# Moving the second weights' extremes from the front into the row loop, and quantizing in half pieces

## The chip, the cores and the metric

The kernel runs on one core of a Trainium2 chip. The metric is the device time of one execution in microseconds. Three runs of the kernel before took 2254.0, 2258.8 and 2258.85 us; the median is 2258.8 us. One further execution was profiled; it took 2269.5 us.

## The reference

The input is eight images of 256 channels and 56 x 56 points. Layer 0 normalizes `x` in groups of eight channels, computes from it a 7 x 7 kernel for every point and each of 16 groups (an involution), applies it and adds the result to `x`. Layer 1 normalizes again, and applies two 3 x 3 convolutions with batch norm and residuals. Both convolutions have ternary weights, and these are what the change is about:

```python
def ternary_quantize(x):
    mx, mn = (jnp.max(x), jnp.min(x))
    lo = mn + (mx - mn) / 3
    hi = mx - (mx - mn) / 3
    return jnp.where(x < lo, -1.0, jnp.where(x > hi, 1.0, 0.0)).astype(x.dtype)

def noised_tri_conv(x, w):
    tw = w - jnp.mean(w)
    tq = ternary_quantize(tw)
    out = lax.conv_general_dilated(x, tq, ...)
    center = tq[:, :, 1, 1]
    extra = lax.stop_gradient(jnp.einsum("bchw,oc->bohw", x, center))
    return out + extra
```

Each weight tensor (256 x 256 x 3 x 3, 2.36 MB) needs its mean, its maximum and its minimum before any of its values can be quantized. The quantized weights are first used by the convolutions, after layer 0 is complete.

## The kernel before, in words

The kernel has three stages: layer 0 (`ph1`), the two convolutions (`ph2`, one after the other) and a final pass over all images (`ph4`). The change touches only `ph1`.

**The row loop.** Layer 0 works through 32 quarters: eight images `b` of four quarters `c` of 64 channels. A quarter has ten rows `ty` of tiles, so the loop has 320 rows. For a row, TensorE multiplies the tiles `q` of the input with the kernels `a` of this quarter (`apply_row`, L815, PSUM tile `pa`), ScalarE and VectorE bring the result out (L827 and L828, tile `inv`), and GpSimd adds it to `x` in place (L831). In the same row, `generate` makes one or two of the fourteen units of the next quarter's `a`: TensorE matmuls into `pg` (L782), ScalarE (L786) and VectorE (L791) add the bias `bt` and write `a`. `pg` has two PSUM homes. Tiles `q` come half from a DMA (L742, four homes, fetched four rows ahead, each waiting for the row whose home it takes) and half from a transpose in TensorE (L749). Further steps are spread over the rows: the statistics of the next image (`gn1_stats`) and of this one (`gn2_stats`), both L150; loads of the next image (L545); stores of the finished one (L843); the shifted copies of the next image (`prep`, with stores at L708); and `params`, which computes the normalization of the next image from row 20 of its predecessor on, one step at each of two places in a row, with the bias matmul `br` (L576) and the addition `brn` (L579) as its last two steps.

**The order.** `pin` fixes the order of every engine's instructions to that of the text. DMAs on SyncE (SP) are in the order of the text too: one that waits holds up those behind it. Some DMAs are put into the list `tasks` and issued by `transfer(2)` at the start of the next row.

**Extremes.** Before the loop, in the front, both weights are loaded into one large tile `wf` (L631), which later is a home of `a`. `extremes` takes each weight tensor in six pieces of 768 columns: VectorE reduces to maximum (L208) and minimum (L209), ScalarE to the sum (L210). Then come small reductions, two matmuls and a transpose that bring the values of the 128 partitions together (L213 to L230), and the thresholds (L232 to L245). Behind the loads of `wf`, SP writes zeros from the tile `xn` to the borders of the scratch tensors `xtd` (L637); GpSimd writes the first shifted copy of image 0 into the same `xn` (L674), so it waits for these.

**Quantization.** From row 8 of the loop on, `quantize` takes one step in every row. Each weight tensor is taken in sixteen pieces of 3 x 96 columns. A piece has one home in SBUF and takes seven rows: fetch (L257), the two comparisons (L261, L262) two rows later, the subtraction and first combination (L264 to L277) in the next, then five more combinations of 96 columns in two rows (L279 to L284), and a store of six planes through `tasks` (L287). Both tensors take 224 rows.

Of the kernel before, what the change touches and what calls it, by code (L numbers as in the profile page):

```python
# [80 lines left out]

QN, QJ = 96, 3 * C // 96
QS = WT
SLOT = (0, 2, 3, 4, 5, 1)
QM = 6


@with_exitstack
def involution_tri_block_kernel(
# [102 lines left out]
    def piece_of(pool, name):  # L192
        return pool.tile([P, (4 + QS) * QN], F32, tag="piece", name=f"piece_{name}")

    def extremes(w, cols, pool, transposer, psum_tile, name):

# [6 lines left out]

        s, mx, mn = col(QM), col(QM), col(QM)
        f = nf // QM
        for j in range(QM):
            v = w[:, j * f:(j + 1) * f]
            nc.vector.tensor_reduce(mx[:, j:j + 1], v, AX.X, ALU.max)  # L208
            nc.vector.tensor_reduce(mn[:, j:j + 1], v, AX.X, ALU.min)  # L209
            nc.scalar.activation(v, v, AF.Identity, accum_out=s[:, j:j + 1])  # L210
            yield
        sums, ends = col(), col(2)
# [5 lines left out]
        nc.vector.memset(v[:, :P], 1.0)  # L218
        yield

        ps = psum_tile(f"ends_{name}")
        nc.tensor.matmul(ps[:, P:P + 1], v[:, :P], sums, start=True, stop=True)
        nc.tensor.transpose(ps[:2, :P], ends, transposer)
        mean, top = cols[:, 0:1], col()
        nc.vector.tensor_scalar(mean, ps[:, P:P + 1], 1.0 / (P * nf), None, ALU.mult)
        nc.vector.tensor_reduce(top[:2], ps[:2, :P], AX.X, ALU.max)
        nc.vector.tensor_copy(v[:2, P:2 * P], top[:2].to_broadcast([2, P]))
        yield
        ps = psum_tile(f"all_{name}")
        nc.tensor.transpose(ps[:, :2], v[:2, P:2 * P], transposer[:2, :2])  # L230
        ex = col(2)
        nc.vector.tensor_copy(ex, ps[:, :2])  # L232
# [4 lines left out]

        d, q0, r, th = (col() for _ in range(4))
        nc.vector.tensor_tensor(d, amx, amn, ALU.subtract)
# [7 lines left out]

    def quantize(dst, w_dram, cols, pool, tasks, name):


        mean, lo, hi = (cols[:, k:k + 1] for k in range(3))
        for t in range(CT):
            for j in range(QJ):
                v = piece_of(pool, name)
                w, u = v[:, :3 * QN], v[:, 3 * QN:]
                o = (t * QJ + j) * 3 * QN
                nc.sync.dma_start(w, w_dram[:, o:o + 3 * QN])  # L257
                yield
                yield
                g = u[:, :3 * QN]  # L260
                nc.vector.tensor_scalar(g, w, mean, hi, ALU.subtract, ALU.is_gt)  # L261
                nc.vector.tensor_scalar(w, w, mean, lo, ALU.subtract, ALU.is_lt)  # L262
                yield
                nc.vector.tensor_tensor(g, g, w, ALU.subtract)  # L264

                def part(x, k):
                    return x[:, k * QN:(k + 1) * QN]


                c0, c1 = max(C, j * QN) - j * QN, min(2 * C, (j + 1) * QN) - j * QN  # L270
                if c0 < c1:
                    g1 = part(u, 0)[:, c0:c1]
                    nc.vector.tensor_scalar(g1, g1, 2.0, None, ALU.mult)

                e, f = part(w, 0), part(w, 1)
                g1, g0, g2 = (part(u, k) for k in range(3))
                nc.vector.tensor_tensor(e, g0, g2, ALU.add)  # L277
                yield
                nc.vector.scalar_tensor_tensor(f, g2, 4.0, g0, ALU.mult, ALU.add)  # L279
                nc.vector.tensor_tensor(part(u, 3), e, g1, ALU.add)  # L280
                nc.vector.tensor_tensor(part(u, 4), e, g1, ALU.subtract)
                yield
                nc.vector.scalar_tensor_tensor(part(u, 5), g1, 2.0, f, ALU.mult, ALU.add)
                nc.vector.scalar_tensor_tensor(part(u, 6), g1, -2.0, f, ALU.mult, ALU.add)  # L284

                def store(u=u[:, QN:], o=t * 3 * C + j * QN):
                    nc.sync.dma_start(  # L287
                        bass.AP(dst[:].tensor, dst[:].offset + o,
                                [[QS * CT * 3 * C, P], [CT * 3 * C, QS], [1, QN]]), u)

                tasks.append(store)
                yield
                yield

# [223 lines left out]
    with ExitStack() as ph1:  # L518
# [38 lines left out]
        def params(b):  # L557


            dst = small.tile([P, NCQ, 2], F32, tag="gn1", name=f"gn1_{b}")  # L560
            yield from group_norm_params(mvs.pop(b), dst, ps_one, f"a{b}")
            for c in range(NCQ):
                nc.vector.tensor_scalar(
                    wrn[:, c, :].rearrange("p (i r) -> p i r", i=2),
                    wr[:, c, :].unsqueeze(1).to_broadcast([P, 2, CR]),
                    dst[:, c, 0:1], None, ALU.mult)

            edge = small.tile([P, 2, NCQ], F32, tag="gn1e", name=f"gn1e_{b}")
            for j in range(2):
                nc.vector.tensor_scalar(edge[:, j], dst[:, :, 1], side_sb[:, j:j + 1], None, ALU.mult)  # L570
            prm[b], prm_edge[b] = dst, edge
            yield
            ps = ps_one(f"br_{b}")
            for c in range(NCQ):
                for i in range(2):
                    nc.tensor.matmul(ps[i * CR:(i + 1) * CR, :1], wr[:CH, c, :], dst[:CH, c, 1:2],  # L576
                                     start=(c == 0), stop=(c == NCQ - 1))
            yield
            nc.vector.tensor_tensor(brn, br, ps[:, :1], ALU.add)  # L579
# [43 lines left out]
        for v in xe:  # L623
            nc.gpsimd.memset(v, 0.0)

        nf = CT * 9 * C
        wf = apool1.tile([P, A_COLS], F32, tag="a1", name="wf")
        for i, v in enumerate((w1, w2)):
            for j in range(2):
                o = j * nf // 2  # L630
                nc.sync.dma_start(wf[:, i * nf + o:i * nf + o + nf // 2], v[:, o:o + nf // 2])  # L631
        zero = xn.rearrange("p k r x -> p (k r x)")

        for d in (d for ds in xt_d for d in ds):
            for r0, n in ((0, PAD), (PAD + HH, HQ - PAD - HH)):
                e = n * QX * RP // P
                nc.sync.dma_start(  # L637
                    bass.AP(d[:].tensor, d[:].offset + r0 * QX * RP, [[e, P], [1, e]]), zero[:, :e])

        def reduce(b, py):  # L640
# [251 lines left out]
        for _ in params(0):  # L892
            pass
        strips, around = prep(0), surround(0, 0)
        a_next = matrices(0)
        thresholds = [pieces.tile([P, 32], F32, tag=f"cols{i}", name=f"cols{i}") for i in range(2)]
        ext = [extremes(wf[:, i * nf:(i + 1) * nf], thresholds[i], pieces, ident_sb, ps_one, f"w{i}")
               for i in range(2)]

        found = chain(*(islice(v, QM) for v in ext), *ext)  # L900

        for py in range(PY):
            next(strips)
            transfer(len(tasks))
            reduce(0, py)
            for _ in range(3):
                next(found)
# [25 lines left out]
        for k in rows[:QLEAD]:  # L933
            transpose_q(*k)
        pin()
        norm = iter(())
        quant = chain(*(quantize(wq_d[i], v, thresholds[i], pieces, tasks, f"w{i + 1}")
                        for i, v in enumerate((w1, w2))))
        last = None
# [197 lines left out]
```

## Time and profile before

| what | us |
|---|---|
| median of three runs | 2258.8 |
| the profiled execution | 2269.5 |
| its span, first to last instruction | 2267.7 |
| first full row of `apply_row` matmuls starts | 80.67 |
| the first convolution's matmuls start | 1155.95 |
| PE, DVE, ACT, POOL busy | 1866.4, 1706.7, 1268.3, 584.5 |
| mean granted TensorE clock | 0.924 |

The span is what the profile shows of the profiled execution; all times of single instructions count from its start. A share of busy time is a mean over stages with different limits. Where an engine is idle, the profile names the event that ended its wait. A granted clock of 0.5 means that TensorE ran at half speed. GB/s and the DMA share are means over the stretch asked for.

### The profile page before, as it was taken

The page shows a single profiled execution, that of the slowest core. Times are in us where ns is not written, and L with a number is a line of the kernel's source. Part 1 is how long each engine was busy: PE and PEld are TensorE (multiplying, and loading weights), DVE is VectorE, ACT ScalarE, POOL GpSimd, SP SyncE. Part 2 cuts the span into 40 slices and gives each one's busy share as a digit, 9 for nine tenths or more (in the row PEclk, how much of TensorE's full clock was granted, in tenths as well). Part 3 has the DMA queues.
Part 4 walks back from the last instruction along what each step waited for, and adds up shares of the span by engine and source line. Part 5 has one row for each costly group of instructions (what it writes and reads, how often), then busy time and mean ns, then how long its engine had stood idle before and what let it go on. Part 6 is the DMA issues. An engine that isn't in the chain of part 4 may idle for free.

```text
span 2267.7 us, 72706 instructions
## 1 busy us (share of the span) xinstructions
PE 1866.4 (82%) x31088; PEld 1716.6 (76%) x31088; DVE 1706.7 (75%) x2906; ACT 1268.3 (56%) x2461; POOL 584.5 (26%) x1320
## 2 busy tenths in 40 slices
PE   4889899898998989999879999999799999970000
PEld 3778777777877877778779999999799999970000
DVE  6676857667585775655689999998999999975444
ACT  3555455455554645556446766665576666673434
POOL 2545546364563645546400000000000000000000
PEclk9899999999999999999989999999899999995555
DMA  6556646566474754645453333334333333369999
GB/s 211 154 157 181 199 131 206 147 192 189 131 221 120 225 164 138 197 119 160 138 206 116 129 134 140 119 116 161 133 138 117 116 116 116 116 255 401 410 430 403
DMA packets 156447, 411.24 MB, mean 181 GB/s; under 512 B 51550, under 2 KB 62172, under 8 KB 148444
## 3 DMA queue, kind: packets, MB, share of 16 engines
q1 hardware_dynamic: 150528, 376.56, 49.9%
q10 hardware_dynamic: 5596, 30.03, 3.2%
q8 instruction: 245, 4.01, 0.8%
q14 instruction: 78, 0.64, 0.1%
HBM read 264.05 MB, written 142.48 MB: 179 GB/s over the span
## 4 chain that ended last, share of the span: by engine, by line
PE 38%; DMA 7%; DVE 3%; ACT 1%; issue 1%; ACTq 0%; SPq 0%; POOL 0%; DVEq 0%
PE c L464 37%; DMA y1f<-y1d 3%; DMA x1f<-x1d 2%; DMA out_y<-x1f 1%; DVE x1f L1064 1%; DMA y2f<-y2d 1%; ACT dummy L416 1%; DVE y1f L1062 0%; ACT y1f L1061 0%; ACT y1f L1063 0%; PE pa L815 0%; PE ptq L749 0%; DVE q L346 0%; DVE r L366 0%; DVE u L373 0%
## 5 line engine op out<-in xcount | busy, mean ns | idle before, releaser
L464 PE MATMUL c<-pl,wq 128*128 128x392 f32 x4608 | 857.1, 348 | 20.2 <-ACT pl L351 20.2
L464 PEld LDWEIGHTS c<-pl,wq 128*128 128x128 f32 x4608 | 855.1, 189 | 22.0 <-ACT pl L351 20.7
L791 DVE TENSOR_TENSOR a<-pg,bt 126x756 f32<-126x756 f32 (+3 forms) x640 | 393.2, 656 | 192.7 <-ACT a L786 147.3
L782 PE MATMUL pg<-kr,wl 64*126 64x140 f32 (+1 forms) x6144 | 459.4, 294 | 14.3 <-DVE a L791 7.1
L782 PEld LDWEIGHTS pg<-kr,wl 64*126 64x126 f32 x6144 | 396.8, 196 | 66.4 <-issue 41.5
L815 PE MATMUL pa<-a,q 126*32 126x48 f32 x17920 | 273.2, 208 | 62.3 <-issue 38.5
L815 PEld LDWEIGHTS pa<-a,q 126*32 126x32 f32 x17920 | 223.1, 111 | 115.8 <-issue 53.4
L786 ACT ACTIVATE a<-pg,bt 126x126 f32<-126x126 f32 x768 | 243.3, 475 | 102.6 <-PE pg L782 102.4
L831 POOL TENSOR_TENSOR x<-x,inv 128x168 f32<-128x168 f32 x320 | 166.4, 520 | 438.5 <-DVE inv L828 375.5
L828 DVE SCALAR_TENSOR_TENSOR inv<-pa,half_sb,inv 128x168 f32<-128x168 f32 x320 | 117.1, 366 | 171.0 <-ACT inv L827 144.8
L351 ACT CAST pl<-r 128x812 fp32r<-128x812 f32 x192 | 162.5, 868 | 145.2 <-DVE r L346 126.9
L752 ACT COPY q<-ptq 126x384 f32<-126x384 f32 x320 | 138.2, 481 | 162.7 <-issue 96.2
L331 POOL MEMSET xp<- 128x116 f32 x32 | 6.3, 195 | 829.4 <-DVE a L346 829.4
L416 ACT ACTIVATE dummy<-y,nc 128x1568 f32<-128x1568 f32 (+2 forms) x144 | 210.1, 1459 | 5.3 <-DVE y L484 3.5
L674 POOL TENSOR_SCALAR xn<-x,gn 128x224 f32<-128x224 f32 (+2 forms) x384 | 179.1, 486 | 130.0 <-PE pt L717 70.8
L352 DVE TENSOR_TENSOR pl<-r,pl 128x812 fp32r<-128x812 f32 x192 | 187.2, 1002 | 28.2 <-ACT pl L351 27.0
L674 POOL TENSOR_SCALAR xe<-x,gn 128x168 f32<-128x168 f32 (+2 forms) x384 | 161.2, 439 | 0.0
L720 ACT COPY stg<-pt 98x512 f32<-98x512 f32 x128 | 74.9, 585 | 137.0 <-issue 88.5
L749 PE MATMUL ptq<-ident_sb,xe 128*126 128x128 f32 x960 | 144.2, 285 | 4.6 <-DVE var_a L170 2.6
L150 DVE BATCH_NORM_STATS2 st<-x 128x6 f32<-128x392 f32 x256 | 138.3, 557 | 11.8 <-DMA x<-in_x 10.2
L827 ACT ACTIVATE inv<-pa,half_sb 128x168 f32<-128x168 f32 x320 | 128.2, 401 | 26.8 <-PE pa L815 25.7
L1011 ACT ACTIVATE xp<-raw,gn 128x392 f32<-128x392 f32 (+1 forms) x124 | 82.6, 721 | 62.9 <-DVE a L346 58.9
(144 smaller groups left out, 1846.2 us busy)
## 6 DMA issues: line engine op xcount, KB each, us to landing
q<-xtd SPq DMA_DIRECT2D x320, 252.0 KB
raw<-x1d SPq DMA_DIRECT2D x32, 812.0 KB
raw<-y1d SPq DMA_DIRECT2D x32, 812.0 KB
x<-in_x SPq DMA_DIRECT2D x64, 392.0 KB
xtd<-stg SPq DMA_DIRECT2D x128, 196.0 KB
x1d<-x SPq DMA_DIRECT2D x64, 392.0 KB
y1d<-y SPq DMA_DIRECT2D x30, 784.0 KB
y2d<-y SPq DMA_DIRECT2D x30, 784.0 KB
```

What stands on the lines that cost most here:

```text
L150: nc.vector.bn_stats(st[:, j, :], xt[:, j * NC:(j + 1) * NC])
L351: nc.scalar.copy(hi, r)
L352: nc.vector.tensor_tensor(lo, r, hi.bitcast(F32), ALU.subtract)
L416: nc.scalar.activation(dst, v, f, bias=shift[:, to:to + 1], accum_out=stats[:, to, j, n:n + 1])
L464: nc.tensor.matmul(ps[:, to, :NM], wq[k][:, t, dx, to * P:(to + 1) * P], part[:, t, :, dx:dx + W], start=(c == 0), stop=(c == last))
L674: nc.gpsimd.tensor_scalar(dst[:, i - d - k0:f - d - k0, :, x0:x0 + n], v[:, i:f, :, j0:j0 + n], scale, bias, ALU.mult, ALU.add)
L749: nc.tensor.transpose(pt[:NQ, k * P:(k + 1) * P], xe[c % 2][:, k, PY * ty:PY * ty + QY].rearrange("p r x -> p (r x)"), ident_sb)
L782: nc.tensor.matmul(dst, wl[rows, c, gp, o:o + NQ], kr[py][rows, px, :], start=True, stop=True)
L786: nc.scalar.activation(whole[:, g0 + i, p0 + j], ps[:NQ, i, j * nt:(j + 1) * nt], AF.Identity, bias=bt[:, c, g0 + i, p0 + j:p0 + j + 1])
L791: nc.vector.tensor_tensor(dst[:, g0:g0 + 2, p0:p0 + nv].rearrange("q g p t -> q g t p"), ps[:NQ, :, t0 * nv:t1 * nv].rearrange("q i (t p) ...
L815: nc.tensor.matmul(ps[o:o + 32, k * 2 * n:(k + 1) * 2 * n], q[:NQ, k, o:o + 32], av[:, t + k, g * 2 * n:(g + 1) * 2 * n], start=True, stop ...
L831: nc.gpsimd.tensor_tensor(xv, xv, iv.rearrange("p t (y x) -> p y t x", x=PX), ALU.add)
```

## The change

It has three parts.

1. The second weights leave the front. Only the first tensor is loaded into `wf`, and its load stands behind the zero writes in SP's order. Its six pieces go two to each of the three steps `py` in front of the first `generate`, its small steps between the first units. The second tensor's extremes stand in the loop between the quantization of the first and of the second: twelve pieces of 384 columns are fetched into the piece homes, and VectorE makes all three reductions, maximum and minimum in one row and the sum in the next. ScalarE has no part in it. Two pieces take five rows, the whole 36 steps.
2. Pieces of the quantization have 48 columns for 96, and there are two homes for one. The work of a half piece is in two rows for four: the comparisons, the subtraction and the first combination in one, the five others in the next. Two half pieces take seven rows, three rows apart, so one tensor takes 115 steps. The store is issued by SP in its place in the row and no longer through `tasks`, three rows after the last of its work on VectorE. One row after it comes the fetch into the same home.
3. `params` has one more empty step ahead of the bias matmul `br`; this and `brn` come half a row later in the text.

```diff
-QN, QJ = 96, 3 * C // 96
+QN, QJ = 48, 3 * C // 48
-QM = 6
+QM, QM2 = 6, 12
     def piece_of(pool, name):
-        return pool.tile([P, (4 + QS) * QN], F32, tag="piece", name=f"piece_{name}")
+        return pool.tile([P, (4 + QS) * QN], F32, tag="piece", bufs=2, name=f"piece_{name}")
+    def paced(events):
+        for r in range(max(events) + 1):
+            for f in events.get(r, ()):
+                f()
+            yield
...
+        def fetch(j):
+            held[j] = piece_of(pool, name)[:, :f]
+            nc.sync.dma_start(held[j], w_dram[:, j * f:(j + 1) * f])
+        def seek(j):
+            v = w[:, j * f:(j + 1) * f] if w is not None else held[j]
             nc.vector.tensor_reduce(mx[:, j:j + 1], v, AX.X, ALU.max)
             nc.vector.tensor_reduce(mn[:, j:j + 1], v, AX.X, ALU.min)
-            nc.scalar.activation(v, v, AF.Identity, accum_out=s[:, j:j + 1])
-            yield
+            if w is not None:
+                nc.scalar.activation(v, v, AF.Identity, accum_out=s[:, j:j + 1])
+        def add(j):
+            nc.vector.tensor_reduce(s[:, j:j + 1], held.pop(j), AX.X, ALU.add)
+        events = {}
+        for j in range(n):
+            if w is not None:
+                events[j] = [lambda j=j: seek(j)]
+            else:
+                r = 5 * (j // 2) + j % 2 * 2
+                events.setdefault(r, []).append(lambda j=j: fetch(j))
+                events.setdefault(r + 2, []).append(lambda j=j: seek(j))
+                events.setdefault(r + 3, []).append(lambda j=j: add(j))
+        yield from paced(events)
...
+        events = {}
+        for k in range(CT * QJ):
+            r = 7 * (k // 2) + k % 2 * 3
+            for n, f in ((0, fetch), (2, ternary), (3, planes_of), (6, store)):
+                events.setdefault(r + n, []).append(lambda f=f, k=k: f(k))
+        yield from paced(events)
...
             prm[b], prm_edge[b] = dst, edge
             yield
+            yield
             ps = ps_one(f"br_{b}")
...
-        nf = CT * 9 * C
-        wf = apool1.tile([P, A_COLS], F32, tag="a1", name="wf")
-        for i, v in enumerate((w1, w2)):
-            for j in range(2):
-                o = j * nf // 2
-                nc.sync.dma_start(wf[:, i * nf + o:i * nf + o + nf // 2], v[:, o:o + nf // 2])
         zero = xn.rearrange("p k r x -> p (k r x)")
         for d in (d for ds in xt_d for d in ds):
...
+        nf = CT * 9 * C
+        wf = apool1.tile([P, A_COLS], F32, tag="a1", name="wf")
+        for j in range(2):
+            o = j * nf // 2
+            nc.sync.dma_start(wf[:, o:o + nf // 2], w1[:, o:o + nf // 2])
...
-        found = chain(*(islice(v, QM) for v in ext), *ext)
+        found = ext[0]
         for py in range(PY):
             next(strips)
             transfer(len(tasks))
             reduce(0, py)
-            for _ in range(3):
+            for _ in range(2):
                 next(found)
...
-        quant = chain(*(quantize(wq_d[i], v, thresholds[i], pieces, tasks, f"w{i + 1}")
-                        for i, v in enumerate((w1, w2))))
+        made = [quantize(wq_d[i], v, thresholds[i], pieces, f"w{i + 1}")
+                for i, v in enumerate((w1, w2))]
+        quant = chain(made[0], ext[1], made[1])
```

In the new `quantize`, `ternary` holds the lines L261 to L277 of before, `planes_of` L279 to L284 and `store` L287, each over half as many columns.

## The prediction

> **What bounds the kernel now.** I read the page first, then the timeline of the front (0 to 90 us), then stretches of the loop, then the groups by shape and the waits. On the page:
>
> ```profile
> PE 1866.4 (82%) x31088; PEld 1716.6 (76%) x31088; DVE 1706.7 (75%) x2906; ACT 1268.3 (56%) x2461; POOL 584.5 (26%) x1320
> ```
>
> PE is the fullest engine, but the share hides three stages: a front until the first row's matmuls (80.67 us), the row loop (to 1147 us), and the two convolutions with the final pass, which the change doesn't touch. In the front PE waits for others. The timeline from 0 to 45 us (start, length, engine, line, work, idle time ahead and its releaser):
>
> ```profile
> 12.02 5.13 SPq L631 DMA_DIRECT2D wf<-in_w  x4
> ...
> 17.27 16.56 SPq L637 DMA_DIRECT2D xtd<-xn  x16
> ...
> 35.59 1.34 POOL L674 TENSOR_SCALAR xn<-x,gn 128x224 f32<-128x224 f32 x3 [31.85 <-DMA xtd<-xn]
> ...
> 36.98 1.09 PE L717 MATMUL pt<-ident_sb,xn 128*98 128x128 f32 x4 [5.59 <-POOL xn L674]
> ```
>
> Both weights (4.7 MB) go out ahead of the sixteen zero writes that read `xn`; POOL can't overwrite `xn` before these land, and PE idles 5.59 us. From 45 to 90 us:
>
> ```profile
> 56.38 0.84 ACT L210 ACTIVATE wf<-wf 128x768 f32<-128x768 f32 x1 [1.02 <-DVE cols L209]
> ...
> 59.83 0.56 PE L222 MATMUL ends_w<-cols,piece_w 128*128 128x1 f32 x2 [3.28 <-DVE piece_w L218]
> ...
> 80.67 0.80 PE L815 MATMUL pa<-a,q 126*32 126x48 f32 x54 [1.03 <-DVE a L791]
> ```
>
> The extremes of the second weights stand in the middle of this, and PE waits behind them. In the loop, two stretches of 40 rows (one image), the first with quantization, the second without (us, then PE, PEld, DVE, ACT, POOL busy, clock, DMA share, GB/s):
>
> ```profile
> 353.10:491.00 137.90, 122.93 (x3312) 104.72 (x3310) 96.67 (x237) 73.64 (x201) 72.62 (x160) 0.99 0.58 169
> ...
> 904.90:1040.10 135.20, 124.35 (x3312) 106.57 (x3310) 81.95 (x179) 72.97 (x201) 69.95 (x160) 0.96 0.55 157
> ```
>
> PE is at 90%. Quantization adds 14.7 us to DVE and 2.7 us to the image: most of it hides behind PE, not all.
>
> **What the Trainium skill says.** Its page "TensorE: Matmul & The Clock Gate", part 1, says that an idle window of about 3.4 us halves the PE clock. The trace agrees: after the 5.59 us gap the record has 0.5 from 33.8 to 40.6 us, and again from 57.7 to 64.5 us around the 3.28 us gap. "VectorE: DVE Perf Modes", on the TRN2 errata, says each SBUF operation pays a fixed latency, so many small tiles pay it each time. The trace agrees: back to back, 96 columns start 167 ns apart, of which 100 would be columns at 0.96 GHz. "DMA: Bandwidth & Descriptors", Queues, rings and completion order, has descriptors consumed in ring order. Here the first weight packet starts at 16.6 us when `x` ends (17.7), and zeros run from 28.1 to 34.9, after the weights.
>
> **The front, step by step.** The zeros now stand directly behind `x`: 17.7 plus the 5.9 us that they took behind the weights is 23.6 us, so POOL may write `xn` at about 24.3 instead of 35.59. The first weights (2.36 MB at the 410 GB/s of 18 to 28 us) follow until 29.4 us, their first half until 26.5. DVE then has six pieces of two reductions, 0.86 us apart: 10.3 us from 27.2, done at 37.5. ACT needs the first two pieces at 32.3, when DVE has done them (30.6), and the last two at about 43. So PE runs the first `pk` as before until 31.4, `pt` at once, two `pk` of 3.67 us (the warm length of the third) with ACT's 2 x 1.03 us of sums between, and the first `pg` at about 42 instead of 47.27: 5.3 us won. Then twelve reductions' tail, four leftover pieces and one tail of two are gone. The first five `pg` follow at the POOL-PE pace of 2.2 us that stands in the trace, the next nine at what two PSUM slots allow (`pg` 1.15, ACT 1.25, DVE 0.7 or ACT 0.75, DVE 1.0: some 3.7 us a pair against 6 to 8 before). The last DVE `a` ends at 66, and the first row's `pa` stands at about 68 instead of 80.67. I take a gain of 12.5 us. Bounds: 9 (one more cold window and the weights 2 us late) to 15 (no slack lost at any hop).
>
> **The loop, step by step.** Groups of DVE by shape (busy us, then mean ns of one, then idle time ahead), 100 to 1150 us:
>
> ```profile
> L264 DVE TENSOR_TENSOR piece_w<-piece_w 128x288 f32<-128x288 f32 x32 | 15.8, 494 | 0.0
> L261 DVE TENSOR_SCALAR piece_w<-piece_w,cols 128x288 f32<-128x288 f32 x32 | 15.2, 475 | 0.1
> ```
>
> and a reduction of the front, from the same view of 20 to 80 us:
>
> ```profile
> L208 DVE TENSOR_REDUCE cols<-wf 128x1 f32<-128x768 f32 x12 | 11.5, 955 | 0.0
> ```
>
> These overlap at their ends, so I count from start to start (medians in the timeline): 460, 345 and 485 ns for the three 288-column operations, 63 for the doubling (126, in half of the pieces), 175 for `e`, five of 167: 2.36 us a piece; 5.7 pieces an image give 13.5, near the 13 to 15 us above. Half as many columns saves 150 ns (144 columns at 0.96 GHz) or 50 (48) each: 310 + 195 + 335 + 45 + 125 + 5 x 117 = 1.60, and the ternary's subtraction now directly follows the comparison it needs, about 0.1 more. Two halves cost 3.4 us for 2.36: 32 x 1.03 = 33 us more DVE. The second extremes add 36 reductions over 384 columns at 860 - 400 = 460 ns: 16.6 us, and a tail of 24 small ones at 0.15: 3.5 us. ACT's sums of it go (6 x 1.03 us), counted in the front. Together 53 us more DVE, in rows 8 to 273 of 320 where quantization now ends at row 231 (115 + 36 + 115 steps for 112 + 112).
>
> What is it worth? The four stretches of one image give 137.9, 137.9 and 136.8 us with, 135.2 without: 2.3 us for 13.8 us of DVE, 0.17. The one without had a clock of 0.96, the others 0.97 on average; allowing for it gives 0.28. Setting row times (start to start of L827's output copies) against the DVE piece work of the same and the three rows before, each of the 40 row kinds against its own mean, gives 0.19 with a standard error of 0.17. I take 0.2: 10.6 us. Below: 0.1, 5 us. Above: in the quarters with the next image's statistics DVE has 25 of 32 us already and gets 27, PE's own work is 27; there most of it could show, 0.4 overall, 21 us.
>
> The second extremes' four matmuls and the wait for their PSUM slots by the next `ptq` cost about 1 us.
>
> **What costs nothing, and why.** SP:
>
> ```profile
> SPq L287 <- DVE st L150: 49.1, 17, 4.4
> ...
> SPq L257 <- DMA wqd<-piece_w: 31.1, 20, 3.4
> ```
>
> The store no longer stands ahead of a row's loads waiting for DVE: its DVE work is three rows old, so that wait goes. The fetch still waits for the store of its home, now issued one row before and not one and a half; stores took 2.2 to 5.4 us from issue to last packet, mostly under 4, a row 3.4, so SP stands up to 2 us, 64 times. Behind it are the next row's transfers and `q` load, which is wanted four rows (13 us) later; without this cover each microsecond would be 64 us. Stores double their packets (24,576 more, 22 to 24 ns each over 16 engines: 34 us of DMA time in 900 us at a share of 0.58); below nothing is not excluded, above 3 us. The same DMA page, Specifications, wants 512 B for full rate, but 384 B was under that too. The fetch has two rows until DVE's comparison; if late, DVE's `inv` and `a` stand behind it.
>
> The bias matmul: the order of PE's instructions does not change there, since nothing of PE stands between the two places. PE's wait for DVE's chain stays:
>
> ```profile
>   DVE gn L173: 15.0, 9
> ```
>
> That is 1.64 us at most of the eight places. Only the small addition `brn` moves behind two `a` operations; it is read some three rows later, by ACT's copies of the next image's `pk`. Cost and gain nothing.
>
> **Sum.** -12.5 + 10.6 + 1 = -0.9 us. It is made against the profiled execution (2269.5 us, span 2267.7), which is 10.7 us over the median of the three runs; nothing in either term scales with that, so I put it on the median: 2258 us.
>
> **Rivals.** (1) The loop hides nearly all: 0.05 to 0.1 of 53 us. For it: DVE idles 1.0 us of 3.45 in a quantizing row; against it: the 2.3 us above. -12.5 + 4 + 0 = -8.5, with the better fronts to -12: 2249. (2) VectorE becomes the bound in the two quarters of each image that carry statistics: 0.4 of 53 is 21 us, and 21 + 1 - 12.5 = +9.5: 2268. It turns slower than the 0.3% bound (6.8 us) from a share of 0.35 up. For it: 27 us of DVE against 27 of PE there; against: the regression puts it one error away. (3) The front keeps only 6 us, for the clock falls cold again or the weights hold ACT: 2265. (4) The bias step does remove its gap, 7 x 1.64 = 11.5 us more: 2247; the unchanged PE order speaks against it.
>
> **Numbers.** A difference of 0.3% is about what a measurement of this kernel tells from none. Forecast 2258 (own range 2251 to 2265): 0.47. Rival 1: 0.22. Rival 2: 0.23. Rival 3: 0.05. Rival 4: 0.03. Faster 0.26, same 0.48, slower 0.26. The range for 8 in 10 takes in most of rivals 1 and 2: 2247 to 2270.
>
> **What would show it.** Zeros issued ahead of the weights and POOL's first `xn` near 24 us; the first row's `pa` near 68 us; DVE busy up by about 50 us in rows 8 to 273; rows of the statistics quarters longer by about 1 us a quarter; the wait before the bias matmul still 1.6 us. It is wrong if the first `pa` stays over 72 us, if the loop grows by less than 5 or more than 18 us, or if SP's fetch waits show in PE's waits for `q`.

## The result and the profile after

The kernel after took 2255.8 us in the median (2246.9 to 2265.3), the kernel before 2258.8 us beside it (2249.0 to 2269.8): a ratio of 0.9982, with an interval of 0.9964 to 0.9999, or 4.1 us less (0.2 to 8.1). A second measurement gave 0.9993 (0.9976 to 1.001), 1.6 us less. By the bound of 0.3% that is no difference, as forecast, and the forecast time of 2258.0 is 2.2 us off. Behind it stand two terms of opposite sign, a gain in the front and a cost in the loop. The gain was put 5.9 us too small, and by the timed runs the cost was put too small as well.

On the page of the kernel after, the line of busy times and the costliest group that gained idle time (busy us, mean ns of one, then the idle time of PE ahead of the group, and the event that ended most of it):

```profile
PE 1852.5 (82%) x31088; PEld 1704.3 (76%) x31088; DVE 1751.4 (78%) x3226; ACT 1262.9 (56%) x2449; POOL 579.3 (26%) x1320
...
L822 PE MATMUL pg<-kr,wl 64*126 64x140 f32 (+1 forms) x6144 | 448.7, 289 | 25.2 <-DVE a L831 13.9
```

and the same group on the page of the kernel before:

```profile
L782 PE MATMUL pg<-kr,wl 64*126 64x140 f32 (+1 forms) x6144 | 459.4, 294 | 14.3 <-DVE a L791 7.1
```

DVE has 44.7 us more and 320 instructions more. PE has the same work in fewer busy microseconds, because less of it ran at half clock; it waits longer for DVE's `a` ahead of `pg`.

**The front.** The timeline of the kernel after from 0 to 72 us (start, length, engine, line, work, idle time ahead and its releaser):

```profile
12.61 11.15 SPq L671 DMA_DIRECT2D xtd<-xn  x16
...
23.80 0.92 SPq L678 DMA_DIRECT2D wf<-in_w  x2
...
24.67 5.63 PE L691 MATMUL pk<-x,wrn 64*128 64x280 f32 x32
...
25.56 1.33 POOL L714 TENSOR_SCALAR xn<-x,gn 128x224 f32<-128x224 f32 x3 [21.81 <-DMA xtd<-xn]
...
29.50 0.95 DVE L223 TENSOR_REDUCE cols<-wf 128x1 f32<-128x768 f32 x1 [4.55 <-DMA wf<-in_w]
...
30.23 0.64 PE L757 MATMUL pt<-ident_sb,xn 128*98 128x128 f32 x4
...
30.80 3.67 PE L691 MATMUL pk<-x,wrn 64*128 64x280 f32 x32
...
38.67 0.91 PE L822 MATMUL pg<-kr,wl 64*126 64x140 f32 x12
...
60.72 1.53 DVE L831 TENSOR_TENSOR a<-pg,bt 126x504 f32<-126x504 f32 x2 [1.68 <-ACT a L826]
...
62.31 0.80 PE L855 MATMUL pa<-a,q 126*32 126x48 f32 x54 [1.03 <-DVE a L831]
```

The zeros go out ahead of the weights, POOL writes `xn` 10.0 us earlier, `pt` follows at 30.23 without PE's gap of 5.59 us, and the first full `pa` starts 18.36 us earlier. The stretches of the two parts of the front, up to the first `pg` and from there to `pa`, of the kernel before (us, then PE, PEld, DVE, ACT, POOL busy, clock, DMA share, GB/s):

```profile
24.40:47.30 22.90, 17.17 (x108) 12.82 (x106) 15.76 (x20) 9.70 (x21) 4.01 (x9) 0.85 0.47 164
47.30:80.70 33.40, 24.54 (x236) 20.13 (x238) 21.77 (x62) 16.64 (x45) 15.14 (x36) 0.80 0.32 95
```

and of the kernel after:

```profile
24.70:38.70 14.00, 13.88 (x108) 10.91 (x106) 9.44 (x13) 8.00 (x16) 4.01 (x9) 1.00 0.53 188
38.70:62.30 23.60, 18.61 (x230) 15.17 (x228) 15.97 (x40) 13.57 (x37) 15.11 (x36) 1.00 0.44 135
```

8.9 us are won up to `pg` and 9.8 us after it. Nearly the same PE work takes 9.2 us less busy time, and PE idles 9.5 us less: half of the gain is pace, half is gaps. The clock column (0.85 and 0.80 before, 1.00 after) leaves one thing out. The record of the clock begins at 30.4 us before and at 27.9 us after, and the view counts what lies ahead of it as full speed; yet the first `pk` ran at half pace there: its pairs of matmuls start 460 ns apart up to that point and 233 ns from it on. In the fourteen profiles this point lies anywhere from 27.9 to 31.4 us, so about 1 us of the front's gain belongs to these two executions. In the second profiles of both kernels the first full `pa` stands at 81.58 and 62.83 us, 18.75 us apart.

**The loop.** The stretch from the `inv` copy of row 8 to that of row 280 of the kernel before, with the columns of the last two views:

```profile
105.80:1040.10 934.30, 846.08 (x22512) 723.66 (x22510) 633.00 (x1522) 499.38 (x1363) 486.35 (x1085) 0.97 0.59 169
```

and of the kernel after:

```profile
87.00:1027.20 940.20, 844.21 (x22516) 720.73 (x22514) 690.12 (x1872) 498.70 (x1363) 481.15 (x1085) 0.98 0.62 171
```

DVE has 57.1 us more in these rows and the rows take 5.9 us longer, at a mean clock of 0.98 for 0.97. PE's waits in the same stretch, before (line, what released it: us in total, times, longest):

```profile
PE pa L815 <- DVE a L791: 15.4, 20, 1.4
...
PE pk L651 <- DVE a L791: 8.7, 9, 1.2
...
PE pg L782 <- DVE a L791: 4.0, 10, 0.8
PE ptq L749 <- DVE var_a L170: 2.6, 4, 0.9
```

and after:

```profile
PE pa L855 <- DVE a L831: 16.5, 20, 1.4
...
PE pk L691 <- DVE a L831: 9.5, 10, 1.2
PE pg L822 <- DVE a L831: 9.3, 14, 1.3
...
PE ptq L789 <- DVE var_a L170: 4.9, 5, 1.3
PE pg L822 <- DVE piece_w L315: 4.6, 5, 1.2
PE pk L691 <- DVE piece_w L315: 1.8, 3, 0.6
```

With 0.3 us for `piece_w` before, these waits for DVE went from 31.0 to 46.6 us. In the second profiles the same waits went from 33.7 to 46.7 us, and the rows from 935.4 to 937.6. Most of the growth is at `pg` and `pk` in the first pair. DVE's `a` empties `pg`'s PSUM homes, and it comes later when DVE has pieces to do in between. Against it PE's idle time at `pa` that ends with "issue" is 6.6 us less (34.5 us before, 27.9 after). The convolutions and the final pass take the same in both: 428 to 429, 428 to 429, and 239 to 240 us.

### The profile page after: what moved, and what is told of

It reads as the page before. It is cut to its first block, busy times and chain, and to the rows that moved or that the text cites. A ratio compares the mean times of both kernels' runs of the same rounds, so it can differ in the third digit from the quotient of the medians.

```text
span 2253.6 us, 73166 instructions
## 1 busy us (share of the span) xinstructions
PE 1852.5 (82%) x31088; PEld 1704.3 (76%) x31088; DVE 1751.4 (78%) x3226; ACT 1262.9 (56%) x2449; POOL 579.3 (26%) x1320
## 4 chain that ended last, share of the span: by engine, by line
PE 38%; DMA 7%; DVE 3%; ACT 1%; issue 1%; SPq 0%; ACTq 0%; POOL 0%; DVEq 0%
PE c L504 38%; DMA x1f<-x1d 2%; DMA y2f<-y2d 2%; DMA y1f<-y1d 2%; DVE x1f L1104 1%; DMA out_y<-x1f 1%; ACT dummy L456 0%; DVE y1f L1102 0%; ACT y1f L1103 0%; PE pa L855 0%; ACT y1f L1101 0%; SPq L1100 0%; PE ptq L789 0%; DVE q L386 0%; DVE u L413 0%
## 5 line engine op out<-in xcount | busy, mean ns | idle before, releaser
L822 PE MATMUL pg<-kr,wl 64*126 64x140 f32 (+1 forms) x6144 | 448.7, 289 | 25.2 <-DVE a L831 13.9
L822 PEld LDWEIGHTS pg<-kr,wl 64*126 64x126 f32 x6144 | 386.2, 191 | 77.1 <-issue 44.0
L826 ACT ACTIVATE a<-pg,bt 126x126 f32<-126x126 f32 x768 | 243.6, 476 | 103.6 <-PE pg L822 103.3
L789 PEld LDWEIGHTS ptq<-ident_sb,xe 128*126 128x126 f32 x960 | 103.1, 142 | 19.4 <-DVE var_a L170 6.7
```

The source lines that it names most:

```text
L789: nc.tensor.transpose(pt[:NQ, k * P:(k + 1) * P], xe[c % 2][:, k, PY * ty:PY * ty + QY].rearrange("p r x -> p (r x)"), ident_sb)
L822: nc.tensor.matmul(dst, wl[rows, c, gp, o:o + NQ], kr[py][rows, px, :], start=True, stop=True)
L826: nc.scalar.activation(whole[:, g0 + i, p0 + j], ps[:NQ, i, j * nt:(j + 1) * nt], AF.Identity, bias=bt[:, c, g0 + i, p0 + j:p0 + j + 1])
```

## The experiments

Each kernel was measured beside the kernel before on the same chip. First the readings, then what each was for. "Rows" is the time of rows 8 to 280 as above, "DVE" its busy time in them, "half clock" the time in them with a granted clock of 0.5, all in us, from one profiled execution each.

| kernel | medians: its own, of before | ratio (interval) | first full `pa` | rows | DVE | half clock |
|---|---|---|---|---|---|---|
| before | | | 80.67 | 934.3 | 633.0 | 51.2 |
| before_again | 2262.8, 2260.1 | 1.0001 (0.9986–1.0017) | 81.58 | 935.4 | 632.6 | 58.0 |
| after | 2255.8, 2258.8 | 0.9982 (0.9964–0.9999) | 62.31 | 940.2 | 690.1 | 41.0 |
| after_again | 2258.2, 2259.9 | 0.9993 (0.9976–1.001) | 62.83 | 937.6 | 689.1 | 47.8 |
| e1_zeros_first | 2256.2, 2260.1 | 0.9956 (0.9931–0.998) | 75.85 | 925.6 | 632.3 | 41.0 |
| e3_half_only | 2267.9, 2260.1 | 1.0025 (1.0011–1.0039) | 80.92 | 937.8 | 670.6 | 47.8 |
| e2_full_pieces | 2245.9, 2260.1 | 0.9905 (0.9884–0.9925) | 62.83 | 925.4 | 649.3 | 30.7 |
| e2_again | 2249.7, 2259.9 | 0.9956 (0.994–0.9972) | 63.43 | 932.5 | 648.2 | 47.8 |
| e7_split_ops | 2253.8, 2259.9 | 0.9963 (0.995–0.9976) | 62.80 | 937.0 | 674.4 | 47.8 |
| e8_split_dma | 2252.2, 2259.9 | 0.9974 (0.996–0.9989) | 63.22 | 936.0 | 650.3 | 47.8 |
| e9_front_only | 2245.5, 2262.4 | 0.9914 (0.9887–0.9942) | 62.89 | 922.5 | 631.1 | 41.0 |
| e4_planes_twice | 2270.0, 2262.4 | 1.0029 (1.0015–1.0042) | 62.30 | 960.2 | 732.9 | 51.2 |
| e5_no_quant | 2241.8, 2262.4 | 0.9884 (0.9857–0.9911) | 62.96 | 929.2 | 574.5 | 41.0 |
| e6_bias_back | 2253.9, 2262.4 | 0.9957 (0.9934–0.9981) | 62.39 | 940.2 | 689.6 | 44.4 |

A kernel read twice shows how far a reading holds. The profiled rows of e2_full_pieces and e2_again differ by 7.1 us, with their time at half clock, and their ratios have intervals that don't overlap. Ratio and medians of one row can differ too: 0.9956 is 9.9 us for e1_zeros_first, while its medians are 3.9 apart. So a few tenths of a per cent between two kernels decide nothing by themselves here; I set the trace of the stretch beside them.

### The kernels unchanged

> The kernel before, unchanged, for a second profile and for what two equal kernels differ by. Every theory expects a ratio of 1.000 with an interval of about 0.3% to both sides. The first full row of pa should stand at 80.7 us within 1 us, since nothing in the front depends on chance. Rows 8 to 280 took 934.3 us in the first profile (51 us of them at half clock); they should be within 8 us of that, by how many half-clock windows fall into them.

> The changed kernel, unchanged, for a second profile and beside the others on one chip. First full row of pa at 62.3 us within 1. If its 0.9982 stands, 4 us under before; if the kernel with whole pieces (0.9905) is truly 17 us better, it stays 10 us or more over that one here too. Rows 8 to 280 near 940 us with about 41 us at half clock.

The kernel before against itself gave 1.0001, with its first full `pa` 0.9 us later than in the first profile. The front and the DVE time of the kernel after came out as in its first profile, within 1 us.

### The order of zeros and weights alone

In the kernel before:

```diff
-        for i, v in enumerate((w1, w2)):
-            for j in range(2):
-                o = j * nf // 2
-                nc.sync.dma_start(wf[:, i * nf + o:i * nf + o + nf // 2], v[:, o:o + nf // 2])
         zero = xn.rearrange("p k r x -> p (k r x)")
...
+        for i, v in enumerate((w1, w2)):
+            for j in range(2):
+                o = j * nf // 2
+                nc.sync.dma_start(wf[:, i * nf + o:i * nf + o + nf // 2], v[:, o:o + nf // 2])
```

> The kernel before with the zero writes ahead of both weights in SP's order, and nothing else. If the order of the zeros gives a third of the front's gain (POOL's first xn near 25 us instead of 35.6, the first transpose at 30 instead of 37), the first full row of pa stands near 74 us and the whole is 6 us shorter. Rival: the second weights' work on ACT and DVE in the middle of the front takes it all back; then pa stands near 80 us and nothing is won. Rival: the order alone gives nearly all; then pa stands near 64 us. The loop is as before in all of them.

Timeline of this kernel from 20 to 82 us:

```profile
25.82 1.34 POOL L675 TENSOR_SCALAR xn<-x,gn 128x224 f32<-128x224 f32 x3 [22.07 <-DMA xtd<-xn]
...
42.16 0.98 PE L783 MATMUL pg<-kr,wl 64*126 64x140 f32 x12 [1.49 <-ACT kr L657]
...
56.61 0.56 PE L222 MATMUL ends_w<-cols,piece_w 128*128 128x1 f32 x2 [3.91 <-DVE piece_w L218]
...
75.85 0.80 PE L816 MATMUL pa<-a,q 126*32 126x48 f32 x54 [0.80 <-DVE a L792]
```

and its stretch from the first `pg` to `pa`, with the columns of before:

```profile
42.20:75.90 33.70, 21.71 (x236) 17.61 (x240) 25.22 (x66) 17.20 (x45) 15.19 (x36) 0.90 0.33 95
```

POOL has `xn` as early as in the kernel after, and `pg` starts 5.1 us earlier than before. From there to `pa` nothing is won (33.7 us against 33.4): the second weights' reductions still stand there, PE waits 3.91 us behind them, and the clock falls to 0.5 once more. Half clock fills 6.8 us of this stretch, against 13.7 us before, and PE is busy 2.8 us less; the stretch is no shorter for it. So the order gives about 5 of the 18.4 us, and, by difference, leaving the second weights out (with two pieces of the first to a step for three) gives the other 13. The medians show 3.9 us; of the ratio's 9.9 us (4.5 to 15.6) the near end alone fits the 4.8 us of the front.

### Half pieces alone, and the rest without them

The first has the whole of the change's part 2 (48 columns, two homes, the paced steps, the store in its place in the row) in the kernel before. The second has all but this of the kernel after: `quantize` of before, one home, and the second extremes fetched in six pieces of 768 columns, each reduced as two halves, one fetch in seven rows.

```diff
-QN, QJ = 48, 3 * C // 48
+QN, QJ = 96, 3 * C // 96
-                r = 5 * (j // 2) + j % 2 * 2
+                r = 7 * (j // 2) + j % 2 * 2
```

> The kernel before with the quantization in half pieces with two homes, and nothing else: front as before (pa at 80.7 us), both extremes in front. If DVE time costs 0.25 us per us, 33 us more of it give 8 us: ratio 1.0035, rows 8 to 280 longer by 8 us. Rival: covered by PE, ratio 1.000 and rows within 3 us. Rival: the taken-away wait of SP wins something: ratio under 0.999.

> The changed kernel with the quantization of before (pieces of 96 columns, one home, store through tasks); the second extremes stay in the loop, 768 columns fetched at once into the one home and reduced in halves. First full row of pa at 62.3 us as in the changed kernel. If the loop is paid for by DVE time at about 0.25 us per us, the halves' 33 us are worth 8 us: rows 8 to 280 take 5 us more than before, not 14, and the whole is 12 us under before (2247). Rival: the halves cost nothing, and the second extremes' steps (or their matmuls) make all of the loop's loss: then it is like the changed kernel, 4 us under before. Rival: the halves with two homes are a gain, by taking away SP's waits for DVE: then it is slower than the changed kernel.

> The kernel with whole pieces and the second extremes in the loop once more, to tell its lead over the changed kernel from chance. Theory: 0.990 to 0.994, 10 to 17 us under the changed kernel. Rival, that its first reading was luck with half-clock windows (31 us of them in rows 8 to 280 against 41 to 58 elsewhere): 0.995 to 0.997, within 7 us of the changed kernel.

Half pieces alone cost 5.7 us by the ratio (2.5 to 8.8) for 37.6 us more DVE. Their rows are 3.5 us longer, with 3.4 us less at half clock, where 8 us were expected. Without them the kernel is at 2245.9 and 2249.7 us in two readings, below the kernel after in both. That is 14.2 and 10.2 us under the kernel before by the medians, 21.5 and 9.9 by the ratios. The second ratio, 0.9956, lies in the range that the rival of luck had named (0.995 to 0.997): the lead over the kernel after is 17 us by the first pair of ratios and 8 us by the second. The stretch of rows of the first profile:

```profile
87.30:1012.80 925.50, 838.81 (x22517) 716.47 (x22515) 649.33 (x1576) 499.44 (x1364) 488.15 (x1085) 0.98 0.59 173
```

DVE has 40.8 us less than in the kernel after. This is the fastest of the kernels here that compute everything: the whole gain of the front is kept, and DVE gets 16 us more than before instead of 57.

### What of the half piece costs: operations or transfers

Both start from e2_full_pieces. The first makes every DVE operation of `quantize` two over half of its columns, in the same rows; the second makes every fetch and store two DMAs (192-byte runs in the store).

```diff
-                nc.vector.tensor_tensor(g, g, w, ALU.subtract)
+                def vt(out, x, y, op):
+                    halves(lambda o, a, b: nc.vector.tensor_tensor(o, a, b, op), out, x, y)
...
+                vt(g, g, w, ALU.subtract)
```

```diff
-                nc.sync.dma_start(w, w_dram[:, o:o + 3 * QN])
+                for h in range(2):
+                    nc.sync.dma_start(w[:, h * 144:(h + 1) * 144],
+                                      w_dram[:, o + h * 144:o + (h + 1) * 144])
```

> The kernel with whole pieces, but each VectorE operation of the quantization done as two over half the columns; fetches, stores and rows stay. About 35 us more DVE busy in rows 8 to 280 than with whole pieces (684 for 649). If DVE time is what half pieces cost, it is as slow as the changed kernel, 6 to 17 us over whole pieces, and PE's gaps in these rows grow by 5 to 8 us. Rival, that SP's waits and the doubled packets cost it: like whole pieces, within 3 us.

> The kernel with whole pieces, but each fetch and each store as two DMAs of half the columns (144 columns, runs of 192 B), VectorE as with whole pieces. If DVE time is the cost of half pieces, nothing changes against whole pieces (within 3 us). Rival, that the doubled packets (24,576 more) and DMAs cost it: 6 to 17 us over whole pieces.

Split operations bring 26 us more DVE and rows 4.5 us longer than e2_again at the same half clock; split transfers no DVE and rows 3.5 us longer. Beside e2_again, on the same chip, the times are 4.1 and 2.5 us longer by the medians, 1.6 and 4.1 by the ratios, whose intervals overlap. The rows of the split operations fit the price below (26 us at 0.2 are 5.2); a cost of the smaller transfers of 2 to 4 us is not excluded and not shown. Neither kernel reaches the 6 to 17 us that were expected of one of the two. How the cost of the half pieces divides between operations, transfers and the rest of part 2 (two homes, other rows, the store's place) stays open.

### The second extremes left out

From e2_full_pieces, without the second weights' extremes anywhere; the second tensor is quantized with the first one's thresholds, so this part of the computation is left out.

```diff
-        made = [quantize(wq_d[i], v, thresholds[i], pieces, tasks, f"w{i + 1}")
+        made = [quantize(wq_d[i], v, thresholds[0], pieces, tasks, f"w{i + 1}")
...
-        quant = chain(made[0], ext[1], made[1])
+        quant = chain(*made)
```

> The front of the changed kernel with the loop of the kernel before: quantization in whole pieces with one home, and no extremes of the second weights anywhere (left out; its quantization takes the first weights' thresholds). If the 18.4 us of the front reach the end, the whole is 18 us shorter: ratio 0.992 (0.990 to 0.994). Rival: the loop gives part of the front's gain back whatever it carries (a later stage that waits for something fixed in time); then 0.995 or more, with rows 8 to 280 longer than 935 us at the same half-clock time.

With DVE at 631 us as before, the kernel is 19.5 us (13.1 to 25.6) faster: the 17.8 us of its front reach the end. The second extremes in the loop, the difference to e2_full_pieces, are 17 to 18 us of DVE. What they cost in time is not settled: by the medians 2.7 and 6.7 us in the two readings of e2_full_pieces, by the ratios -2.0 and 9.5.

### More and less work on VectorE

The first is the kernel after with five operations of `planes_of` done twice. The second is the kernel after with no quantization on DVE: the quantized weights are left out, and GpSimd clears the six planes that the stores read.

```diff
-            nc.vector.scalar_tensor_tensor(f, g2, 4.0, g0, ALU.mult, ALU.add)
+            for _ in range(2):
+                nc.vector.scalar_tensor_tensor(f, g2, 4.0, g0, ALU.mult, ALU.add)
...
```

```diff
-            nc.vector.tensor_scalar(g, w, mean, hi, ALU.subtract, ALU.is_gt)
-            nc.vector.tensor_scalar(w, w, mean, lo, ALU.subtract, ALU.is_lt)
-            nc.vector.tensor_tensor(g, g, w, ALU.subtract)
...
+            nc.gpsimd.memset(held[k][:, 3 * QN:], 0.0)
```

> The changed kernel with the five last combinations of each half piece done twice: about 37 us more of DVE in rows 8 to 280 (726 for 690), with the same DMAs and order. At 0.15 us per us it is 5 to 6 us slower than the changed kernel (ratio to before near 1.001); if DVE is near its limit and the price rises, 10 us or more. Rival, that DVE time costs nothing and only DMAs do: as the changed kernel, 0.9985.

> The changed kernel without VectorE's part of the quantization: GpSimd writes zeros into each half piece instead, fetches and stores stay (left out: the quantized weights, so the convolutions multiply by zero[...]; only the loop is read). About 105 us less DVE in rows 8 to 280. At 0.15 us per us these rows are 14 to 16 us shorter than the changed kernel's at the same half-clock time; rival, that DMAs cost it: within 4 us of it.

The doubled planes: stretch of rows, and PE's waits in it.

```profile
87.10:1047.30 960.20, 849.97 (x22518) 724.23 (x22516) 732.91 (x2192) 500.39 (x1364) 482.87 (x1085) 0.97 0.61 167
```

```profile
PE pa L856 <- DVE a L832: 16.6, 20, 1.3
PE pg L823 <- DVE a L832: 16.4, 23, 1.4
PE pk L692 <- DVE a L832: 11.6, 14, 1.2
...
PE ptq L790 <- DVE var_a L170: 5.1, 5, 1.4
```

42.8 us more DVE made the rows 20.0 us longer. The time is 16 us longer than that of e6_bias_back, which ran on the same chip and differs from the kernel after only in the bias step, and 11 and 8 us longer than that of the kernel after by its two ratios. PE's wait for `a` ahead of `pg` is the one that grew most, from 9.3 us (7.2 in the second profile) to 16.4 us.

The kernel without quantization on DVE is not clean, since its 64 `memset` and all its DMAs stay. With 115.6 us less DVE than the kernel after its rows are 11.0 us shorter, and no shorter than those of e9_front_only with 57 us more. Either DVE work below some 630 us in these rows costs next to nothing, or the added `memset` and the transfers cost what it saves; the run doesn't tell.

**The price.** I fitted the rows of the table, without the doubled planes and the kernel without quantization (twelve profiles), as a constant plus a share of DVE plus a share of the half clock, by least squares: 928.6 us, plus 0.198 (standard error 0.029) for each us of DVE above 633, plus 0.53 (0.10) for each us of half clock above 45. The scatter left is 2.3 us. For 57 us of DVE that is 11.3 us. The doubled planes lie 8.5 us above the fit, more than three times the scatter, and are left out of it for that. Against the fitted value of the kernel after and with half clock allowed for, they cost 17 us for 43 us of DVE, 0.39: between 690 of 940 us (73%) and 733 of 960 (76%) the price would be about twice that below. That rests on one profile. By the timed runs above the doubled planes cost 8 to 16 us, 0.19 to 0.37 of their DVE time. So a higher price beyond 73% is suggested, not shown.

Two limits of the price itself. In most of the profiles with much DVE the transfers are doubled too, so 0.198 holds for both together; the split operations, with the transfers of before, give 4.5 us for 26 us, 0.17. And it comes from one execution of each kernel. By the timed runs the loop of the kernel after costs what lies between it and e9_front_only, which has the same front: 15.4 and 17.8 us by the ratios, 13.9 and 15.2 by the medians, for 58 to 59 us of DVE, or 0.24 to 0.30.

### The bias matmul back

The kernel after without the additional empty step in `params`:

```diff
             prm[b], prm_edge[b] = dst, edge
             yield
-            yield
             ps = ps_one(f"br_{b}")
```

> The changed kernel with the bias matmul and its addition back in their places of before. PE's order is the same, so the wait of the bias matmul for VectorE stays at about 1.6 us each, and the whole is like the changed kernel within 3 us. Rival, that the step is worth its seven gaps: 8 to 11 us slower than the changed kernel.

What PE waits for ahead of `br` in the kernel after (us, times), and then in this kernel:

```profile
  DVE gn L173: 15.5, 9
  ACT inv L867: 12.9, 7
```

```profile
  DVE gn L173: 15.4, 9
  ACT inv L866: 12.9, 7
```

The gap is the same with and without the edit (and before: 15.0 us, 9 times), and the rows take 940.2 us in both. The trace shows no gain from the edit. The ratio of this kernel, 0.9957, is below the two of the kernel after by 5.7 and 8.1 us, where at most 3 us were expected; the trace shows no place for that difference, and I leave it open.

## Why the prediction was right or wrong

**The front: right in its mechanism, too small by 5.9 us.** Forecast -12.5 us (9 to 15), measured -18.4 us, outside the bounds. The forecast `pa` at 68 came at 62.31; two places make up the difference.

- First `pg`: forecast 42, measured 38.67, 3.3 us. The first `pk` was taken over from before with its end at 31.4; it took 5.63 us for 6.98 and ended at 30.30, since PE came to full pace earlier in this execution (30.98 in the second profile). And I put 2 x 1.03 us of ACT's sums between the next two `pk`; they ran beneath them, and only the weights of the second of these two waited 0.37 us.
- Last DVE `a` to full `pa`: forecast 2 us (66 to 68). After, the last `a` ends at 62.25, 0.06 us ahead of `pa`, as it did in the kernel before, whose `pa` starts at 80.67:

```profile
79.08 1.53 DVE L791 TENSOR_TENSOR a<-pg,bt 126x504 f32<-126x504 f32 x2 [1.68 <-ACT a L786]
```

The stretch between, from the first `pg` to the last `a`, was forecast at 24 us and took 23.6. That was luck in part: the paces given for it, five units at 2.2 us and nine at 3.7 us a pair, add up to 27.7, while the trace has 2.0 us and 2.7 us a pair.

The cold clock was not a term that the sum missed, for full-speed lengths stand in it from the end of the first `pk` on. What was a little late did no harm: zeros landed for POOL at 25.56 (forecast 24.3), and DVE's first reduction waited for the weights until 29.50 (27.2). Two of the twelve reductions ran past the start of the first `pg`, which didn't wait for them. The alternative that the front keeps only 6 us falls.

The Trainium skill ("TensorE: Matmul & The Clock Gate", part 1) has an idle window of some 3.4 us halve the clock. The traces agree with the length, since the record changes in steps of 3.41 us, but not with the idleness. In the kernel before half speed begins at 33.8, 57.7 and 67.9 us, which is 2.4 us after the start of the gap of 5.59 us (not after its end, as the prediction has it), 1.1 us after the start of the gap of 3.28 us, and just behind one of 1.51 us. In the 3.4 us ahead of each, PE was not idle but busy for 0.99, 1.76 and 1.89 us (columns of the stretches above):

```profile
30.40:33.80 3.40, 0.99 (x8) 0.46 (x6) 3.40 (x5) 2.35 (x6) 0.00 (x0) 1.00 0.92 279
54.30:57.70 3.40, 1.76 (x22) 1.35 (x20) 2.05 (x4) 2.38 (x7) 2.52 (x7) 1.00 0.31 87
64.50:67.90 3.40, 1.89 (x22) 1.36 (x21) 3.12 (x18) 1.19 (x3) 2.41 (x6) 1.00 0.32 102
```

**The loop: right in its size.** Forecast 53 us more DVE at 0.2, 10.6 us; measured 57 us, at the fitted 0.198 11.3 us. Taken bare, the rows grew by 5.9 and 2.2 us in the two pairs of profiles, the second under the 5 us that the prediction named as a sign of being wrong; with the half clock allowed for at 0.53, they grew by 11.3 and 7.6. The timed runs put the cost at 14 to 18 us. All but the bare 2.2 lie in the bounds of 5 to 18. The half pieces alone brought 37.6 us (forecast 33) and the second extremes 17 to 18 us (forecast 20). Halving a small operation saves little: one over 48 columns takes 224 ns in the profile, over 96 columns 305. That agrees with the fixed latency of each SBUF operation in "VectorE: DVE Perf Modes", the TRN2 errata. From start to start the trace has 116 to 119 ns for these, as the forecast 117; the comparisons over 144 columns took 384 and 389 ns, where 310 and 195 (and 0.1 us for a dependence) were forecast. One group of the kernel after by shape:

```profile
L315 DVE SCALAR_TENSOR_TENSOR piece_w<-piece_w 128x48 f32<-128x48 f32 x64 | 14.3, 224 | 0.0
```

and of the kernel with whole pieces:

```profile
L315 DVE SCALAR_TENSOR_TENSOR piece_w<-piece_w 128x96 f32<-128x96 f32 x32 | 9.7, 305 | 0.0
```

Of the alternatives, that the loop hides all would be 0.05 to 0.1 of it, three standard errors or more away; that DVE becomes the bound is at most suggested by the doubled planes. Where the time lies was said wrong in part. From the starts of `inv`, the mean times of an image's four quarters (six images) were 31.9, 32.7, 43.8 and 29.1 us before and 33.0, 30.9, 44.7 and 29.7 after; the second profile of each gives 31.8, 32.1, 43.7, 29.5 and 32.6, 31.1, 44.7, 29.1. The first quarter, with statistics of the next image, grew by about 1 us as said; the second, with statistics too, fell by 1.0 to 1.8, and the third, where `params` and `prep` run, grew by about 1.0 instead.

**What was costed at nothing: right by the trace.** The bias step left its gap as it was; its own experiment, timed, leaves open whether the step costs something. SP's transfers: the fetch does wait more for the store of its home,

```profile
SPq L294 <- DMA wqd<-piece_w: 91.8, 47, 5.4
```

for 31.1 us and 20 times before. That is 2.0 us in the mean, the limit that I gave it, with a longest of 5.4. The waits of the store for DVE fell from 103.6 us (L287) to 24.8 (L323), and no DMA is among the releasers of PE in these rows (in the second profile one is, with 0.6 us). The doubled packets of the stores took 15.2 ns each in the mean for 24.1 of the larger ones, so they added 9.8 us of DMA time and not 34.

**The sum: right in the time, with luck.** With the measured terms it is -18.4 + 11.3 = -7.1 us, and the two profiles differ by 14 us, while the timed ratios say -4.1 (-8.1 to -0.2) and -1.6 (-5.4 to +2.3). The profiled executions of the kernel before were 10.7 and 4.1 us above its medians, those of the kernel after 0.4 and 6.4 below. About 5 of the profiles' 14 us go with the half clock of the rows (51 and 58 us against 41 and 48, at 0.53), which is not the same in two executions of one kernel. The remaining 3 to 5 us between -7 and the ratios are inside the first interval and outside the second. They are about what the timed runs put the loop's cost above the fit (14 to 18 us for 11.3); why the profiles show less of it stays open. So a front 5.9 us better than forecast met a loop some 2 to 6 us dearer than the forecast 11.6, and the two misses cancelled. Setting the sum on the median was harmless; had the front been sized right, the forecast would have been about 2252, a little further from the measured 2255.8 than 2258 is.

## What to carry to other kernels

Where PE idles in a start-up, count not only the gap but what the other engines are still held by and the slower pace of PE around it: here half of the gain was pace. Work that is moved to a second engine beside a 90% busy PE isn't free: here a fifth of it came back as time by the profiles, and up to three tenths by the timed runs. Moving whole work there can pay; cut into smaller operations, the same work keeps that engine busy longer, here by 38 us.

## What was unexpected of the hardware

Half clock occurred also in the middle of the loop, with PE 90% busy: 31 to 58 us of some 930, differing between executions of one kernel (30.7 and 47.8 us in e2's two), and each of them cost about half a microsecond. Two profiled executions of one kernel differed by up to 7 us in these rows, and that is why differences of stretches have been set beside the half clock and not taken bare.

It has a pattern that I had not looked for. In the fourteen profiles half speed begins 164 times in the first 1000 us. In the 3.41 us ahead of it matmuls covered 0 to 66% of the time, and less than 55% in 142 of the 164; of 3606 such windows after which full speed stayed, only 15 were under 55%. So in these traces the clock falls after a window in which PE was busy for no more than about half of the time; it need not have been idle throughout. That the busy share is what the clock follows is read from this agreement; no run tests it. And 84 of the 155 beginnings in the loop lie within 4 us of the start of one of the 98 bias matmuls `br`, where PE waits for VectorE once an image. Two such windows of the kernel after (`br` starts at 131.97 and 270.02 us, half speed at 133.7 and 270.3):

```profile
130.30:133.70 3.40, 1.74 (x33) 1.53 (x32) 2.96 (x18) 1.25 (x4) 0.00 (x0) 1.00 0.86 239
266.90:270.30 3.40, 1.09 (x15) 0.64 (x15) 2.89 (x15) 1.25 (x4) 0.54 (x1) 0.99 0.91 260
```

At the fitted 0.53 for each us of half clock, the wait ahead of `br` costs more than its own 1.6 us; no run here removes it.
